# Two routed expert layers: all blocks of an expert in turn, odd 64 rows as half blocks, and jumps announced to TensorE's sequencer

## The chip, the cores and the metric

The kernel runs on one core of one Trainium2 chip. A core has five engines with an instruction queue each: TensorE (PE, matrix multiplications and transposes by matmul, with results in PSUM), VectorE (DVE), ScalarE (ACT), GpSimd (POOL) and SyncE (SP); sixteen DMA engines move data between HBM and the on-chip memory SBUF. Conditional code is executed by every engine for itself: each holds the condition in a register and jumps, or does not. The metric is the device time of one launch in microseconds (us); lower is better. About the trace: a float32 matmul is recorded as two passes.

## The reference

A stack of eight layers over 625 nodes with 512 features, four graph layers and four feed-forward layers alternating, each `x = x + layer(layernorm(x))`. Two feed-forward layers are routed: every node goes to its two best of eight experts. They are what the change rewrites:

```python
# L1: hidden 1024, bias and relu
topk_vals, topk_idx = jax.lax.top_k(x @ gate_w + gate_b, 2)
weights = sum over k of one_hot(topk_idx) * softmax(topk_vals)
out = sum over e of weights[:, e] * (relu(x @ w1[e] + b1[e]) @ w2[e] + b2[e])

# L3: hidden 1536, gated, no bias
probs = softmax(x @ router_w.T)
gates, idx = jax.lax.top_k(probs, 2); gates = gates / sum(gates)
out = sum over e of combine[:, e] * ((silu(x @ w1[e].T) * (x @ wgate[e].T)) @ w2[e].T)
```

The numbers of nodes per expert follow from the seeded inputs: L1 96, 346, 175, 23, 54, 50, 350, 156; L3 197, 240, 352, 99, 77, 43, 149, 93. The kernel does not know them when it is built.

Another layer the change touches is L1's graph layer, two rounds of graph attention. In it, VectorE also has time, and the degree normalisation of the adjacency matrix `aT` (needed in the graph layers of L2 and L3) can be placed anywhere between.

## The kernel before

Nodes are held as 5 tiles of 125. A routed layer has three parts.

**Routing.** `dispatch` (L514) turns the one-hot choices `o12` of the two best experts into slots. A triangular matmul gives each node its rank in its expert and `tot` the number of nodes. A slot is a place (0 to 127) in a block of 128 rows. Blocks 0 to 7 hold the first 128 rows of experts 0 to 7; rows beyond go to overflow blocks 8 to 16, filled in order of experts. One-hot matrices of place (`ohp`) and block (`ohb`) give by matmuls (`ps_id`) the table `node[place, block]` and, in three bf16 pieces, the weights `gate`. `whose` and `routing` say for each overflow block which expert it belongs to, and how many there are.

**Blocks.** `routed` (L619) works on a ring of 11 chunks of weights, 1 MB each, filled by SP (`refill`). Experts have 4 chunks in L1 (two for w1, two for w2) and 9 in L3 (three pairs for w1 and wgate, three for w2). For a block, POOL gathers its 128 rows from HBM (`fetch`, L667), PE transposes them (`enter`, L674), and for each part c of 512 hidden features `ahead` (L1170 in L1, L1335 in L3) multiplies with the upward weights into `ps_h`, `turn` (L688) transposes the hidden rows and `back` (L697) multiplies with the downward weights into `ps_y`. At its end DVE scales by the gate (L703) and POOL adds the rows to `sums` in HBM by an indirect DMA (L705). All code is emitted in one order per engine: `ahead` of unit n, `turn` of unit n-1, `back` of unit n-2, and the entry of the next block in between, over all first blocks without a gap.

Overflow blocks stand in conditionals nested in each other:

```python
with tc.If(n_over > i):
    run([(E + i, c) for c in range(nch)], i + 1 < NO)
    overflow(i + 1)
```

L1 uses 6 and L3 uses 5 of the 9 that the code holds. For an overflow block SP reads from a register which expert's weights to fetch and loads them once more (L654), by conditional DMAs.

A conditional that is not taken has code of its own: each engine waits until its earlier instructions are complete and then raises the semaphores that the skipped instructions would have raised.

**Beside them.** In L1's first units a list of other work (`fill`) is worked off, three items per unit: copies of `x` into `sums` (`keep`, L738), the experts' second bias for all nodes by five matmuls with the gate weights (`expert_bias`, L472), and the degree normalisation of `aT` for the graph layers of L2 and L3 (`normalise`, L1195).

Of the kernel before, what the change touches and what calls it, by code (L numbers as in the profile page):

```python
# [36 lines left out]
TMORE = 3  # L37
# [6 lines left out]
NB = 17  # L44
NO = NB - E
# [31 lines left out]
def _weights(i):  # L77
# [15 lines left out]
    for e in range(E):  # L93
        a, g = _chunks(i["L3_ffn_w1"][e].T), _chunks(i["L3_ffn_wgate"][e].T)
        for c in range(3):
            w += [a[c], g[c]]
        w += _chunks(i["L3_ffn_w2"][e].T)
# [55 lines left out]
def kernel(  # L153
# [51 lines left out]
    def load(w, src):  # L205
        nc.sync.dma_start(w.rearrange("p k m -> p (k m)"), src)
# [307 lines left out]
    def dispatch(layer, o12, weight, w0, per):  # L514


        with tc.tile_pool(name=f"{layer}d", bufs=1) as dp:
# [4 lines left out]
            rank, tot = ps[:T, 0, :NT * E], ps[:, 1, :E]  # L522
            nc.tensor.matmul(rank, tri, mask.rearrange("p t e -> p (t e)"), start=True, stop=False,
# [6 lines left out]
            for s in range(NT):  # L530
                nc.tensor.matmul(tot, ones16, mask[:, s, :], start=(s == 0), stop=(s == NT - 1))
            gt = dp.tile([P, E, 4], F32, tag="gt", name="gt")
            nc.vector.tensor_tensor(gt, tot[:, :, None].to_broadcast([P, E, 4]),
                                    thr[:, None, :].to_broadcast([P, E, 4]), op=OP.is_gt)
            nov = dp.tile([P, E], F32, tag="nov", name="nov")
            nc.vector.tensor_reduce(nov, gt, axis=AX.X, op=OP.add)
            pm = dp.tile([P, E, E], F32, tag="pm", name="pm")
            nc.vector.tensor_mul(pm, before, nov[:, None, :].to_broadcast([P, E, E]))
            ovb = dp.tile([P, E], F32, tag="ovb", name="ovb")
            nc.vector.tensor_reduce(ovb, pm, axis=AX.X, op=OP.add)  # L540
            delta = dp.tile([P, E], F32, tag="delta", name="delta")
            nc.vector.scalar_tensor_tensor(delta, ovb, float(B), dconst, op0=OP.mult, op1=OP.add)
            rk = rank.rearrange("p (t e) -> p t e", e=E)
            sl = dp.tile([T, NT, E], F32, tag="sl", name="sl")
            nc.vector.scalar_tensor_tensor(sl, rk, float(B),
                                           delta[:T, None, :].to_broadcast([T, NT, E]),
                                           op0=OP.is_ge, op1=OP.mult)
            nc.vector.tensor_add(sl, sl, rk)
            nc.vector.tensor_add(sl, sl, e128[:T, None, :].to_broadcast([T, NT, E]))
# [13 lines left out]
            ohp = dp.tile([T, 2 * NT, B], BF16, tag="ohp", name="ohp")  # L563
            ohb = dp.tile([T, 2 * NT, NB], F32, tag="ohb", name="ohb")
            nc.vector.tensor_tensor(ohb, blk[:T, None, :].to_broadcast([T, 2 * NT, NB]),
                                    bcast(at[:, 1, :], NB), op=OP.is_equal)
            nums = dp.tile([T, 2 * NT, NB, 2], BF16, tag="nums", name="nums")
            num = number.rearrange("p c t i -> p (c t) i")
            for i in range(2):
                nc.vector.tensor_mul(nums[:, :, :, i], ohb, bcast(num[:, :, i], NB))  # L570
            ps = pstile("ps_id")
            for n in range(2 * NT):
                nc.vector.tensor_scalar(ohp[:, n, :], place[:T, :], at[:, 0, n:n + 1], None,
                                        op0=OP.is_equal)
                nc.tensor.matmul(ps[:, 0, :2 * NB], ohp[:, n, :],
                                 nums[:, n].rearrange("p b i -> p (b i)"), start=(n == 0),
                                 stop=(n == 2 * NT - 1))
            one = dp.tile([P, NB], F32, tag="one", name="one")
            nc.vector.tensor_reduce(one, ps[:, 0, :2 * NB].rearrange("p (b i) -> p b i", i=2),
                                    axis=AX.X, op=OP.add)  # L580
            free = dp.tile([P, NB], F32, tag="free", name="free")
            nc.vector.tensor_scalar(free, one, 0.0, spare, op0=OP.is_equal, op1=OP.mult)
            node = small.tile([P, NB], I32, tag="node", name="node")
            nc.vector.scalar_tensor_tensor(node, one, -1.0, free, op0=OP.add, op1=OP.add)

            nc.vector.tensor_add(ovb, ovb, nov)
            le = dp.tile([P, NO, E], F32, tag="le", name="le")
            nc.vector.tensor_tensor(le, ovb[:, None, :].to_broadcast([P, NO, E]),
                                    blk[:, :NO, None].to_broadcast([P, NO, E]), op=OP.is_le)
            own = dp.tile([P, NO], F32, tag="own", name="own")  # L590
            nc.vector.tensor_reduce(own, le, axis=AX.X, op=OP.add)
            nc.vector.tensor_scalar(own, own, float(E - 1), None, op0=OP.min)
            whose = small.tile([P, NO, E], F32, tag="whose", name="whose")
            nc.vector.tensor_tensor(whose, own[:, :, None].to_broadcast([P, NO, E]),
                                    eio[:, None, :].to_broadcast([P, NO, E]), op=OP.is_equal)
            routing[layer] = small.tile([1, NO + 1], I32, tag="own_i", name="own_i")
            nc.vector.tensor_scalar(routing[layer][:, :NO], own[0:1, :], float(per), float(w0),
                                    op0=OP.mult, op1=OP.add)
            nc.vector.tensor_copy(routing[layer][:, NO:], ovb[0:1, E - 1:])

            rest = dp.tile([T, 2 * NT], F32, tag="rest", name="rest")
            nc.vector.tensor_copy(rest, weight)
# [14 lines left out]
        return node, gate, whose  # L617

    def routed(layer, node, gate, nch, nw, hidden, turned, first_fill=(), fill=()):  # L619
# [3 lines left out]
        w0, per = (W_L1, 4) if layer == "L1" else (W_L3, 9)  # L623
        assert state["taken"] == state["loaded"] == state["stop"]
        with tc.tile_pool(name=f"{layer}w", bufs=1) as more, \
# [9 lines left out]
            slots = kpool.tile([P, NT, D], F32, tag="K", name="slots")  # L635
            xgs = [slots[:, n, :] for n in range(3)]
            ys_out = [slots[:, n, :] for n in range(3, 5)]
            xgTs = [rpool.tile([P, KD, B], F32, name=f"xgT{n}") for n in range(2)]
            brought = {"n": 0}
            read = set()  # L640
            first = {}
            hs, hTs, ys = {}, {}, {}

            def bring(n):

                b, j = divmod(n, per)
                if b < E:
                    load(ring[n % RING], weights[w0 + n])
                    return
                if b not in first:  # L650
                    first[b] = nc.sync.value_load(routing[layer][0:1, b - E:b - E + 1],
                                                  min_val=w0, max_val=w0 + per * (E - 1))
                src = weights[bass.ds(first[b] + j, 1)].rearrange("a p m -> (a p) m")
                nc.sync.dma_start(ring[n % RING].rearrange("p k m -> p (k m)"), src,  # L654
                                  cond=n_over > b - E)

            def refill():

                while brought["n"] < NB * per:
                    n = brought["n"]  # L660
                    if n >= RING and n - RING not in read:
                        return
# [680 lines left out]
    def l3_turned(hT, pt, c, b, pool):  # L1343
        evac(hT, pt)
# [35 lines left out]
```

## Time and profile before

| What | Value |
|---|---|
| median of 3 runs (lowest to highest) | 1725.51 us (1724.1 to 1725.95) |
| the profiled execution | 1723.04 us |
| its span in the trace | 1721.1 us |
| granted clock of TensorE over the span | 0.936 of full speed |
| L1: `node` written, first `ps_h`, end of last `ps_y` | 786.2, 793.8, 1018.0 us |
| L3: `node` written, first `ps_h`, end of last `ps_y` | 1271.5, 1282.1, 1708.4 us |
| weights moved, L1 and L3 | 14 x 4 and 13 x 9 chunks of 1 MB |

The page of a profile gives the span, the busy time of each engine, the chain of work that ended last, followed back from the last instruction, and the costliest groups of instructions. A group's line reads: line of the kernel, engine, operation, output and input with their shapes, count, then busy time and mean duration of one in nanoseconds, then the idle time of the engine just before them and what ended it. A row of a table by window gives its bounds and length, each engine's busy time, the granted clock, the busy share of the DMA engines and the GB/s that they moved. A row for one line of the kernel gives shortest, median and longest duration in nanoseconds.

### The profile page before, as it was taken

To read this page: it belongs to the slowest core of one execution; us is meant where nothing else is said; L and a number is where in the kernel's file an instruction comes from. 1 tells how busy PE (TensorE), PEld (TensorE's weight loads), DVE (VectorE), ACT (ScalarE), POOL (GpSimd) and SP (SyncE) were. 2 spreads that over 40 slices of the span, in tenths; PEclk is the share of its full clock that TensorE was granted. 3 is DMA by queue.
4 is the path that set the end of the run, shared out by engine and by line. 5 is a ranking of instruction groups with operands and counts; after the bars stand their busy time and mean duration, and the time that the engine had idled before them with its cause. 6 is when DMAs were issued, how large, how long until landed. Compare 5 with 4: busy or idle time off the path is not lost.

```text
span 1721.1 us, 15559 instructions
## 1 busy us (share of the span) xinstructions
PE 1528.4 (89%) x5642; PEld 861.3 (50%) x5642; DVE 676.1 (39%) x1738; ACT 357.8 (21%) x680; POOL 235.5 (14%) x254
## 2 busy tenths in 40 slices
PE   7996999989897989846999969698759999999997
PEld 5774466555555656533444436354534444444443
DVE  9824562451974168466122225635331111111110
ACT  1102362011661046311111115301211000000100
POOL 2010042010540034101111112001000000000000
PEclk8998999999999989977999989799869999999998
DMA  3000200011001100136889731011258888869871
GB/s 135 16 28 25 73 1 25 31 68 53 22 1 49 49 26 1 40 112 234 302 270 342 256 87 73 25 49 49 102 217 299 301 309 304 307 244 359 311 265 50
DMA packets 40142, 237.12 MB, mean 138 GB/s; under 512 B 4779, under 2 KB 4907, under 8 KB 14299
## 3 DMA queue, kind: packets, MB, share of 16 engines
q1 hardware_dynamic: 30705, 214.80, 33.7%
q0 software_dynamic: 6608, 15.99, 4.1%
q10 hardware_dynamic: 2746, 5.25, 1.0%
q8 instruction: 48, 0.79, 0.2%
q14 instruction: 35, 0.29, 0.1%
HBM read 246.11 MB, written 14.26 MB: 151 GB/s over the span
## 4 chain that ended last, share of the span: by engine, by line
PE 70%; DVE 12%; issue 10%; DMA 4%; ACT 2%; POOL 1%; SPq 0%; POOLq 0%; ACTq 0%; DVEq 0%
PE ps_mf L359 17%; PE ps_y L697 9%; PE ps_h L1335 9%; PE ps_mn L367 7%; PE ps_h L1170 5%; PE ps_s L796 4%; PE ps_eo L496 4%; PE ps_o L860 3%; DMA sumsL<-slots,node 3%; PE ps_p L839 3%; PE ps_tr L328 2%; DVE ln_st L277 1%; DVE s L802 1%; PE ps_t L688 1%; DVE dst L913 1%
## 5 line engine op out<-in xcount | busy, mean ns | idle before, releaser
L1335 PE MATMUL ps_h<-ring,xgT 128*128 128x512 f32 x624 | 274.8, 595 | 0.8 <-DVE xgT L226 0.8
L697 PE MATMUL ps_y<-ring,hT 128*128 128x512 f32 x536 | 239.2, 593 | 0.9 <-issue 0.9
L1335 PEld LDWEIGHTS ps_h<-ring,xgT 128*128 128x128 f32 x624 | 118.7, 191 | 147.9 <-issue 145.3
L697 PEld LDWEIGHTS ps_y<-ring,hT 128*128 128x128 f32 x536 | 97.6, 190 | 103.9 <-issue 103.0
L825 POOL TENSOR_SCALAR s<-s,rs 125x625 f32<-125x625 f32 (+4 forms) x120 | 103.2, 875 | 294.0 <-DVE rs L822 269.9
L705 POOL DMA_INDIRECT sumsL<-slots,node x27 | 42.6, 1578 | 469.3 <-DVE slots L703 358.6
L1338 ACT ACTIVATE g<-ps_h 128x512 f32<-128x512 f32 x39 | 23.3, 597 | 395.6 <-PE ps_h L1335 364.5
L1170 PE MATMUL ps_h<-ring,xgT 128*128 128x512 f32 x224 | 103.2, 609 | 2.1 <-ACT xgT L234 1.3
L807 ACT ACTIVATE s<-s,mn 125x626 f32<-125x626 f32 (+4 forms) x120 | 87.2, 743 | 49.3 <-DVE mn L802 49.1
L802 DVE CUSTOM_DVE_ANT_0 s<-ps_s,mask 125x626 f32<-125x626 f32 (+4 forms) x120 | 82.6, 718 | 29.0 <-PE ps_s L796 27.8
L796 PE MATMUL ps_s<-kT,qT 64*125 64x313 f32 (+4 forms) x416 | 86.4, 466 | 2.8 <-DVE mn L802 2.8
L328 PE MATMUL ps_tr<-ident,xn 125*128 125x125 f32 x140 | 30.2, 398 | 62.6 <-DVE ln_nb L300 49.1
L226 DVE COPY hT<-ps_t 128x512 f32<-128x512 f32 x26 | 18.0, 692 | 171.5 <-PE ps_t L688 171.5
L1340 DVE TENSOR_TENSOR h<-ps_h,g 128x512 f32<-128x512 f32 x39 | 26.8, 686 | 147.9 <-ACT g L1338 147.9
L839 PE MATMUL ps_p<-ident,s 125*125 125x125 f32 x432 | 65.8, 293 | 14.0 <-POOL s L825 11.7
L359 PE MATMUL ps_mf<-xT,w 128*128 128x313 f32 x256 | 69.7, 434 | 6.6 <-ACT xT L402 6.6
L839 PEld LDWEIGHTS ps_p<-ident,s 125*125 125x125 f32 x432 | 53.9, 194 | 40.0 <-POOL s L825 28.6
L1170 PEld LDWEIGHTS ps_h<-ring,xgT 128*128 128x128 f32 x224 | 43.6, 196 | 57.5 <-issue 53.8
L817 DVE SCALAR_TENSOR_TENSOR s<-s,cnt 125x626 f32<-125x626 f32 x80 | 67.3, 863 | 9.9 <-ACT s L807 9.9
L496 PE MATMUL ps_eo<-w,h 128*125 128x512 f32 x160 | 70.6, 592 | 0.0
L860 PE MATMUL ps_o<-pT,v 125*64 125x375 f32 (+2 forms) x448 | 60.1, 413 | 9.0 <-DVE mn L802 4.2
L916 PE MATMUL ps_a<-dst,src 125*128 125x313 f16 x400 | 58.0, 309 | 6.9 <-DVE dst L913 5.3
(345 smaller groups left out, 1994.8 us busy)
## 6 DMA issues: line engine op xcount, KB each, us to landing
ring<-in_weights SPq DMA_DIRECT2D x195, 1024.0 KB
w<-in_weights SPq DMA_DIRECT2D x27, 1024.0 KB
rows_hbm<-xn ACTq DMA_DIRECT2D x2, 1120.0 KB
sumsL<-x ACTq DMA_DIRECT2D x2, 1120.0 KB
out<-sumsL SPq DMA_DIRECT2D x1, 1250.0 KB
x<-in_x SPq DMA_DIRECT2D x1, 1120.0 KB
x<-sumsL SPq DMA_DIRECT2D x5, 224.0 KB
rows<-in_rows SPq DMA_DIRECT2D x1, 1052.0 KB
```

The costliest lines, as they stand in the source:

```text
L359: nc.tensor.matmul(ps[:, half, :HC], w, r[:, half * HC:(half + 1) * HC], start=(n == 0), stop=(n == last))
L367: nc.tensor.matmul(ps[:T, 0, :width], src[:, k, t * T:(t + 1) * T], w[:, k, :width], start=(k == 0), stop=(k == KD - 1 and extra is None))
L496: nc.tensor.matmul(ps[:T, 0, :], h[:, t * T:(t + 1) * T], w, start=(f == 0), stop=(f == len(blocks) - 1))
L697: nc.tensor.matmul(ys[b][:, 0, :], hT[:, j, :], ring[n % RING][:, j, :], start=(c == 0 and j == 0), stop=(c == nch - 1 and j == 3))
L796: nc.tensor.matmul(ps[hh][:T, i, :w], qT[rr, b, t * T:(t + 1) * T], kT[rr, b, i * w:(i + 1) * w], start=True, stop=True)
L802: nc.vector.tensor_tensor_reduce(s[:, hh, :nb * w].rearrange("p (a c) -> p a c", a=nb), ps[hh][:T, :nb, :w], mask[:, t, :nb * w].rearrange ...
L807: nc.scalar.activation(s[:, hh, :nb * w], s[:, hh, :nb * w], AF.Exp, bias=mn[:, hh:hh + 1], scale=-1.0, accum_out=sm[:, hh:hh + 1] if caus ...
L825: nc.gpsimd.tensor_scalar(s[:, hh, :w], s[:, hh, :w], rs[:, hh:hh + 1], 1.0, op0=OP.mult, op1=OP.mult)
L839: nc.tensor.transpose(pp[:T, hh, j * T:(j + 1) * T], s[:, hh, j * T:(j + 1) * T], ident[:T, :T])
L860: nc.tensor.matmul(po[rr, 0, o:n * T], v[:, j, h * DH:(h + 1) * DH], pT[:, hh, j, o:n * T], start=(j == 0), stop=(j == nk - 1))
L1170: nc.tensor.matmul(ps[:, 0, :], xgT[:, k, :], w1[:, k, :], start=(k == 0), stop=(k == KD - 1))
L1335: nc.tensor.matmul(ps[:, i, :], xgT[:, k, :], w[i][:, k, :], start=(k == 0), stop=(k == KD - 1))
```

## The change

Both routed layers are rewritten, with one code for both.

- Experts come in straight line, each with all its blocks while its weights are in the ring. Weights are loaded once: 32 MB instead of 56 in L1, 72 instead of 117 in L3. The loads into chunks that a block has read are conditional: they run in the expert's last block alone. The ring has 12 chunks, and in L3 the order of the nine chunks is another.
- An expert has 48 / 8 = 6 block columns. If the number of its half blocks of 64 rows is odd, the first 64 rows are a half block (`l = 0`); all others are full blocks, `l = 1` and, nested, `l = 2` to `5`. In a half block the hidden features (and the output's) are split in two: two matmuls with stationary tiles of 64 columns and 256 moving columns each, on PSUM partitions 0 to 63 and 64 to 127. Its result goes by half rows (`by_half`) to `sums`.
- For each expert, `enter(e + 1)` transposes the next expert's first rows (128 and 64 of them) before this expert's blocks, and then gathers those of the expert after that. Rows of further blocks are gathered one block ahead, and transposed at the start of their block.
- In each block's code `hint` marks, on TensorE alone, that the jump over the blocks behind it is likely taken. The jumps over a half block and over block 1 have no such mark of their own.
- Counts and oddness of all experts, 16 numbers, are read into registers of all engines at the start of the layer.
- `dispatch`: no overflow table; numbers of nodes in one fp16 matmul instead of two bf16 parts; 48 columns instead of 17; the first gathers are issued as soon as `node` is written. In L3 the softmax over eight is gone: the weights come from the difference of the two best logits, as in L1. L1's second bias is now computed here, with copies on ACT (`added`), and added to `x` at its end.
- The degree normalisation is emitted in the projections of the second round of L1's graph layer, two steps per evacuation.

Taken blocks for these counts: in L1 9 full and 5 half, in L3 11 full and 2 half.

The diff at its core:

```diff
-TMORE = 3
+TMORE = 4
...
-NB = 17
-NO = NB - E
+NL = 6
+NB = E * NL
+BH = B // 2
...
-        for c in range(3):
-            w += [a[c], g[c]]
-        w += _chunks(i["L3_ffn_w2"][e].T)
+        d = _chunks(i["L3_ffn_w2"][e].T)
+        w += [a[0], g[0], a[1], g[1], d[0], a[2], g[2], d[1], d[2]]
...
+    def load(w, src, cond=None):
+        nc.sync.dma_start(w.rearrange("p k m -> p (k m)"), src, cond=cond)
...
+            ci = dp.tile([P, E], I32, tag="ci", name="ci")
+            nc.vector.tensor_scalar(ci, tot, 1.0, float(BH - 1), op0=OP.max, op1=OP.add)
+            odd = dp.tile([P, E], I32, tag="odd", name="odd")
+            nc.vector.tensor_scalar(odd, ci, BH, None, op0=OP.bitwise_and)
...
+            xg(node)
+            routing[layer] = number_of.rearrange("p a e -> p (a e)")
+            nc.vector.tensor_copy(number_of[:, 0, :], tot[0:1, :])
+            nc.vector.tensor_copy(number_of[:, 1, :], odd[0:1, :])
...
+            def fetch(e, node):
+                if e < E:
+                    gather(xg_block, node, e, 1)
+                    gather(xg_half, node, e, 0)
+
+            refill()
+            node, gate, node2, gate2 = dispatch(layer, lg, lambda node: fetch(0, node), bias)
+            _, numbers = nc.values_load_multi_w_load_instructions(routing[layer], min_val=0,
+                                                                  max_val=N)
+            counts, odd = numbers[:E], numbers[E:]
...
+            def enter(e):
+                if e < E:
+                    turned(xg_block, xbT[e % 2])
+                    turned(xg_half, xhT[e % 2])
+                    fetch(e + 1, node)
...
+                    n = 1 if l else 2
+                    self.parts = [(slice(g * B // n, (g + 1) * B // n),
+                                   slice(g * 512 // n, (g + 1) * 512 // n)) for g in range(n)]
+                    self.width = 512 // n
...
+                    self.cond = counts[e] < B * l + BH + 1 if l < NL - 1 else None
...
+                def ahead(self, c):
+                    ps, n = pstile("ps_h"), self.width
+                    for i, w in enumerate(up[c]):
+                        w = chunk_of(self.e, w)
+                        for k in range(KD):
+                            for rr, cc in self.parts:
+                                nc.tensor.matmul(ps[rr, i, :n], self.xT[:, k, :], w[:, k, cc],
+                                                 start=(k == 0), stop=(k == KD - 1))
...
+                def run(self):
+                    read.clear()
+                    read.update(before[0])
+                    brought["n"] = before[1]
+                    for n in range(nch + 2):
+                        if n < nch:
+                            self.ahead(n)
+                        if 1 <= n <= nch:
+                            self.turn(n - 1)
+                        if n >= 2:
+                            self.back(n - 2)
+
+            def hint(e, l):
+                if l < NL:
+                    tc.mark_branch_hint_location(f"{layer}e{e}b{l}", "LikelyTaken",
+                                                 engines=[mybir.EngineType.PE])
+
+            def more(e, l):
+                if l < NL:
+                    with tc.If(counts[e] > B * l - BH, label=f"{layer}e{e}b{l}"):
+                        hint(e, l + 1)
+                        turned(xg_more, xbT[e % 2])
+                        if l + 1 < NL:
+                            gather(xg_more, node, e, l + 1)
+                        Block(e, l).run()
+                        more(e, l + 1)
+
             enter(0)
-            run([(b, c) for b in range(E) for c in range(nch)], True)
-            assert not fill
-            overflow(0)
+            for e in range(E):
+                before = set(read), brought["n"]
+                enter(e + 1)
+                with tc.If(odd[e] > 0):
+                    hint(e, 2)
+                    Block(e, 0).run()
+                with tc.If(counts[e] > BH):
+                    hint(e, 2)
+                    gather(xg_more, node, e, 2)
+                    Block(e, 1).run()
+                more(e, 2)
...
+    routed("L1", lg, ((0,), (1,)), (2, 3), vec("L1_ffn_b1"), b2s[:E, 1, :])
...
+    lg = node_logits(xnT, vec("L3_ffn_router_w"), None, "lg")
+    routed("L3", lg, ((0, 1), (2, 3), (5, 6)), (4, 7, 8))
```

## The prediction

> **What bounds the kernel now.** I read the page first: span, busy time, and the chain that ended last.
>
> ```profile
> span 1721.1 us, 15559 instructions
> PE 1528.4 (89%) x5642; PEld 861.3 (50%) x5642; DVE 676.1 (39%) x1738; ACT 357.8 (21%) x680; POOL 235.5 (14%) x254
> PE 70%; DVE 12%; issue 10%; DMA 4%; ACT 2%; POOL 1%; SPq 0%; POOLq 0%; ACTq 0%; DVEq 0%
> ring<-in_weights SPq DMA_DIRECT2D x195, 1024.0 KB
> ```
>
> TensorE leads. The two routed stages, which the change rewrites, are then cut out by time (columns: window, length, busy time of PE, its loads, DVE, ACT and POOL, granted clock, DMA share, GB/s): L1 is the first three rows, L3 the last three.
>
> ```profile
> 764.00:794.00 30.00, 11.39 (x76) 8.28 (x77) 19.51 (x96) 7.77 (x12) 4.37 (x7) 0.61 0.33 112
> 794.00:915.00 121.00, 119.01 (x340) 56.77 (x341) 34.96 (x73) 17.23 (x42) 15.55 (x13) 0.97 0.87 301
> 915.00:1018.00 103.00, 102.05 (x292) 48.61 (x290) 23.83 (x69) 14.26 (x36) 17.06 (x13) 1.00 0.64 222
> 1245.00:1282.00 37.00, 14.31 (x75) 8.99 (x75) 18.12 (x93) 6.86 (x11) 3.32 (x4) 0.55 0.52 187
> 1282.00:1515.00 233.00, 232.85 (x623) 109.02 (x624) 28.18 (x43) 20.70 (x36) 16.03 (x13) 0.99 0.85 300
> 1515.00:1711.00 196.00, 193.42 (x523) 90.31 (x521) 24.75 (x36) 16.53 (x29) 16.00 (x12) 1.00 0.71 256
> ```
>
> Inside the expert stretches PE is busy 98 to 100% at nearly full clock: DMA, though 64 to 87% busy, isn't the limit, so fewer weight bytes save nothing by themselves. Ahead of each stretch lies a routing stretch at 0.55 to 0.61 clock, in which DVE leads. Next, groups by shape, and the jumps of the conditional blocks:
>
> ```profile
> L1335 PE MATMUL ps_h<-ring,xgT 128*128 128x512 f32 x624 | 274.8, 595 | 0.8 <-DVE xgT L226 0.8
> L697 PE MATMUL ps_y<-ring,hT 128*128 128x512 f32 x536 | 239.2, 593 | 0.9 <-issue 0.9
> L1170 PE MATMUL ps_h<-ring,xgT 128*128 128x512 f32 x224 | 103.2, 609 | 2.1 <-ACT xgT L234 1.3
> L860 PE MATMUL ps_o<-pT,v 125*64 125x250 f32 x240 | 28.7, 379 | 7.0 <-DVE mn L802 4.2 <-ACT pT L841 1.7 <-DVE pT L226 1.1
> L730 PEldq COMPARE_BRANCH  x15: 65/65/3839, 920.3 to 1708.6; - x15
> L730 POOLq INC_SWDGE_SEM  x2: 858/1120/1383, 1019.5 to 1709.7; - x2
> ```
>
> An fp32 matmul is two records, 0.429 us apart at full clock: 0.857 us per 512 columns; a 128x128 transpose takes 0.107. From the first ps_h to the last ps_y, L1's 14 blocks take 224.2 us (793.8 to 1018.0), L3's 13 take 426.3 (1282.1 to 1708.4). From one block's first ps_h to the next's, overflow blocks take 15.4 and 32.66 us; less four entry transposes (0.43) that is 14.97 and 32.2.
>
> [...]the ps_o matmuls of attention (L860) are such pairs on partitions 0 to 63 and 64 to 127; both start within 0.01 us and the next pair 0.21 us later, as long as one 250-column pass; the change of mode shows as about 0.05 us. [...]of 15 branches 13 fall through in 0.065 us, L1's exit over 271 instructions takes 0.352, L3's over 722 takes 3.839. [...]L1's first eight ps_h records took 5.33 us where later ones took 3.43.
>
> **The change, part by part**, for the counts that the seeded inputs give: L1 96, 346, 175, 23, 54, 50, 350, 156; L3 197, 240, 352, 99, 77, 43, 149, 93.
>
> *Fewer rows.* L1's 14 full blocks become 9 full and 5 half; L3's 13 become 11 and 2. A half block's 16 (L1) or 36 (L3) pairs cost 2 x 0.214 us each: 6.9 or 15.4; with transposes (0.4 or 0.6) and about 1.0 of evacuations that nothing covers, as a block no longer overlaps its neighbour, 8.3 and 17.1. So L1: 9 x 14.97 + 5 x 8.3 = 176.2; L3: 11 x 32.2 + 2 x 17.1 = 388.4.
>
> *Entries.* enter(e+1) for the six experts from e2 on: 8 transposes with 128 and 64 rows, 0.64 us: 3.9 per stage. The blocks of `more` (4 in each stage) transpose their rows with no other PE work beside: four transposes 0.43, copy 0.69 (L226), semaphores: 1.7 each, 6.8 per stage.
>
> *Blocks not taken.* The old kernel leaves an If twice; the new one leaves 14 times in L1 and 15 in L3. At L1's exit PE's sequencer branched at 1012.3, but its semaphore event waited until PE's own matmuls were through (1018.08), and it went on at 1018.41. I charge 1.15 us (0.85 dead plus waits refilling the pipe) for the first false block of a run and 0.85 to 0.9 for the others: 7 x 1.15 + 2 x 0.9 + 3 x 0.85 = 12.4 in L1, 7 x 1.15 + 5 x 0.9 + 0.85 = 13.4 in L3 (the false blocks behind the last expert are in both kernels). Bounds: 0.4 to 1.8 each, so 10 to 50 for all.
>
> *The announced jumps* (L1 376 to 385, L3 742 to 756 instructions): once announced, 0.35 as at L1's exit. Even unannounced most lie under the 6 us of queued matmuls that hid L3's 3.8; worth 0 to 10. *The unannounced ones*: a skipped half block is 141 to 148 instructions in L1 and 309 to 319 in L3. The latter happens at six experts (e0, e1, e2, e3, e4, e7) with only entry transposes queued ahead. [...]0 to 3.5 each, 0 to 21; I take 4, since the shorter jump of 271 cost 0.35.
>
> *POOL.* Two gathers per expert, one more in each full block, fewer scatters; on a false block POOL waits for its scatter to land (6.6 us median) and for the increment (0.86 to 1.38). Behind a full block that is covered by 15 us or more. Behind L1's half-only e3, e4, e5 (about 11 us each) landing, increment, two gathers and their landing (7.0 median) come to 17: three stalls of up to 6. I take 8 for L1 (0 to 18), 1 for L3. PE cools in these: 2 per stage. SP, in a false block, waits for its loads to land; only later loads are queued behind it, and at least three chunks are in the ring by then, 5 us of a half block's or 10 of a full block's use against 3.0 to 3.4 us per load: nothing, or about 3 per stage where that cover is gone.
>
> Sums: L1 176.2 + 3.9 + 6.8 + 12.4 + 8 + 2 = 209.3 against 224.2: -14.9. L3 388.4 + 3.9 + 6.8 + 13.4 + 4 + 1 + 2 = 419.5 against 426.3: -6.8.
>
> *The start of each stage.* enter(1) stands ahead of expert 0's blocks, and the gathers of expert 1 wait for expert 0's transposes to free the buffer. Before, L1 goes node 786.2, first landing 791.8, first ps_h 793.8. After: node about 786.7, two gathers down by 794.3, transposes, then two more gathers down by 802, ps_h at 803.5: +9.7. In L3 the first gather took 7.7 us beside ring loads that are now issued earlier, and the softmax is gone: +5 (4 to 9). Reading 16 counts (one value 0.26 to 0.54 us now) hides under the first gather on every engine; uncovered at most 4.
>
> *Elsewhere.* The degree normalisation (21 DVE and ACT steps) moves from L1's first units to the L1-gnn projections of its second layer, under PE work; 0 to +3, I take +1. The bias matmuls move into routing, where PE idles. The ring's 12th chunk and the new order of L3's chunks change what DMA holds in reserve, not a wait: DMA must bring 32 MB instead of 56, and 72 instead of 117. Removed DVE routing steps are in the node times above.
>
> Total: -14.9 - 6.8 + 9.7 + 5 + 1 = -6.0. From the profiled execution (1723.04, span 1721.1 and 1.9 around it) that gives 1717.0; that execution lies 2.5 below the median, and put on the median 1725.5 it is 1719.5. I forecast 1719.
>
> **Rivals.** *Overheads hide* (0.27): false blocks cost 0.5[...]. Minus 13 on drains, 8 + 1 + 4 on stalls, gives 1693 to 1705, say 1698. For it: PE's sequencer ran 6 us ahead. Against: both observed exits drained.
>
> *Skipped half blocks miss* (0.16, slower): [...]21 instead of 4, and L1's three (e0, e1, e6) half that, +5: 1741. It decides from two misses on: beyond the 4 charged, 6 us eat the gain. For it: 722 instructions missed[...]. Against: 271 did not.
>
> *Gathers become the path* (0.15, slower): each false block holds POOL for its scatter at every L1 expert, not three, and PE waits 5 us at six of eight and cools: +24, 1743. Against: the full block's cover.
>
> *The announcement does nothing* (0.04): 1719 to 1729, as worked out.
>
> **How the numbers follow.** The sum stands at 0.38, with its own range of 1708 to 1731. About 0.2% (3.5 us) is what a measurement of this kernel can tell from no change. Of the main case 0.25 lies under 1722, 0.09 within, 0.04 above; the hiding rival is all faster, the misses and the gathers nearly all slower, the last mostly within. Faster 0.53, same 0.12, slower 0.35. Cases of both signs hold most of the chance; 1690 to 1750 leaves 2 in 10 out.
>
> **What would show it.** First ps_h 15 to 20 us after node in L1 and L3, with two rounds of gathers between (right) or 7 to 10 (wrong). Half blocks 8 and 17 us with paired starts 0.21 us apart. PE's branches: announced ones at most 0.4, the odd ones of L3 0.1 to 0.4 (right) or near 3.8 (the miss). PE idle before transposes ended by gathers: 8 us in L1, or over 25. Weight loads 104 with 1 MB landing, DMA share below 0.6. It would be wrong if PE's idle per expert is far from 3 us, or if a chunk of weights is late.

## The result and the profile after

The changed kernel takes 1796.5 us (median of 4 runs, 1790.7 to 1798.5) against 1725.1: the ratio is 1.041, 95% interval 1.038 to 1.043. The forecast was 1719, in a range of 1690 to 1750: 77 us off, and on the other side of the kernel before.

The page of the changed kernel, at its head, its instruction fetches, its costliest group, and the weight loads:

```profile
span 1796.8 us, 17242 instructions
PE 1515.9 (84%) x5966; PEld 865.3 (48%) x5966; DVE 670.8 (37%) x1697; ACT 382.1 (21%) x709; POOL 255.7 (14%) x275
...
q8 instruction: 80, 1.31, 0.3%
...
L761 PE MATMUL ps_h<-ring,xbT 128*128 128x512 f32 x672 | 315.3, 627 | 63.1 <-SPq L854 41.3
...
ring<-in_weights SPq DMA_DIRECT2D x158, 1024.0 KB
```

PE was busy for 12.5 us less than before, in a span 75.7 us longer. The idle time ahead of one group, the upward matmuls, is 63.1 us, and what ended most of it is SyncE's queue at L854, the `If` of the half block. The packets on q8, one of the two queues that the page marks "instruction", rose from 48 to 80. (Of the 158 issues of weight loads, 54 took about 0.08 us where the others took 0.33: they are conditional loads that did not run. 104 ran, as forecast.)

By stage, from the records of the two traces, in us (`node` is taken at the start of the instruction that writes it; the three stretches marked * were forecast at +1 together):

| Stretch | before | after | difference | predicted |
|---|---|---|---|---|
| start to L1's logits transposed (`ps_lt`) | 775.2 | 779.9 | +4.7 | * |
| L1: logits to `node` | 10.8 | 11.4 | +0.6 | +0.5 |
| L1: `node` to first `ps_h` | 7.8 | 18.8 | +11.0 | +9.2 |
| L1: first `ps_h` to last `ps_y` | 224.2 | 225.5 | +1.3 | -14.9 |
| to L3's logits | 241.5 | 240.1 | -1.4 | * |
| L3: logits to first `ps_h` | 22.6 | 27.8 | +5.2 | +5 |
| L3: first `ps_h` to last `ps_y` | 426.3 | 479.9 | +53.6 | -6.8 |
| to the end | 12.7 | 13.4 | +0.7 | * |

So the two starts were forecast nearly right, and the expert stretches were wrong by 16 and 60 us. The windows of these two stretches, first before, then after (columns as in the prediction):

```profile
793.80:1018.00 224.20, 221.26 (x631) 105.59 (x631) 58.99 (x141) 31.48 (x78) 32.81 (x26) 0.99 0.77 265
1282.10:1708.40 426.30, 426.25 (x1144) 199.33 (x1144) 52.08 (x77) 37.23 (x65) 30.42 (x24) 1.00 0.79 282
```

```profile
810.10:1035.60 225.50, 195.03 (x764) 98.27 (x764) 39.28 (x91) 27.62 (x78) 39.68 (x36) 0.94 0.43 133
1303.50:1783.40 479.90, 417.10 (x1288) 197.00 (x1288) 51.22 (x81) 61.44 (x85) 38.44 (x32) 0.93 0.42 148
```

The rows saved are there: PE's busy time falls by 26 us in L1 and 9 in L3, although the granted clock is 0.93 to 0.94 there and was 0.99 to 1.00. Idle time took their place: 63 us of L3's stretch, 30 of L1's. That is 7.9 us per expert in L3, where the prediction named "far from 3 us" as a sign of being wrong. What ended it in L3 is told by TensorE's waits from 1300 to 1790 us (who waits, for whom; sum, times, longest; a q behind an engine's name is its instruction queue, where jumps and semaphores are worked off):

```profile
PE ps_h L761 <- SPq L854: 37.6, 4, 9.8
PE ps_h L761 <- PEq L854: 10.9, 2, 6.1
PE ps_h L761 <- SPq L842: 6.7, 2, 3.8
PE ps_x L718 <- DVEq L842: 5.5, 5, 1.1
```

L842 is the `If` of the nested blocks (`more`), L854 that of the half block. Ahead of experts 1, 2, 3 and 4, whose half block is skipped, PE stands still for 9.8, 9.3, 9.5 and 9.1 us. One of these pauses, ahead of expert 1, in the timeline:

```profile
1373.71 0.33 SPq L206 DMA_DIRECT2D ring<-in_weights  x1
...
1374.78 1.02 PE L718 MATMUL ps_x<-ident,rows_g 128*128 128x128 f32 x8 [1.10 <-DVEq L842]
...
1385.57 2.04 PE L761 MATMUL ps_h<-ring,xbT 128*128 128x512 f32 x2 [9.77 <-SPq L854]
```

The last weight load of expert 0 is issued at 1373.7, when its last chunk has been read. In the DMA view of 1373 to 1386 us, slices of 0.325 us, the engines carry about 400 GB/s and more up to 1379 us and less than 100 from 1384.4 on (rows are gathered and added in it too):

```profile
GB/s 454 403 429 429 429 454 429 479 403 429 429 454 429 403 403 403 378 429 227 353 359 410 271 365 277 227 227 315 353 391 410 265 214 126 164 63 76 25 0 0
```

SyncE's own waits in the same stretch:

```profile
SPq L842 <- SPq L842: 10.2, 5, 4.3
```

Its records fit: in the nested block not taken its semaphore events come at 1375.2, 1377.7, 1380.3 and 1384.5 us, 2.5 to 4.3 us apart, then those of the half block not taken until 1385.5, and PE starts at 1385.6. Each of the four comes within 0.03 us of the end of a landing (1375.16, 1377.65, 1380.24 and 1384.50). So SyncE, skipping a block, waits here until the loads it has issued have landed, and PE's next expert waits for SyncE.

A second wait lies under the first. TensorE's jumps at these places (COMPARE_BRANCH is the instruction that jumps or falls through; rows of L3, from 1285 to 1790 us; shortest, median and longest in ns):

```profile
L842 PEldq COMPARE_BRANCH  x15: 69/351/2166, 1333.0 to 1777.6; - x15
L854 PEldq COMPARE_BRANCH  x10: 75/4219/6570, 1297.9 to 1744.7; - x10
L857 PEldq COMPARE_BRANCH  x15: 82/186/237, 1303.1 to 1777.3; - x15
```

Of the announced jumps taken (L842), seven of eight take 0.35 to 0.37, and the one behind expert 5's half block 2.2. Those over a half block, six of the ten at L854, take 4.9, 5.9, 6.6, 6.2, 6.0 and 3.5 us; within each of the six one packet of 16 KB starts on q8 (that the jump waits for it is not shown). In the timeline above TensorE's jump ran from 1375.1 to 1381.0, still inside SyncE's wait.

### The profile page after: what moved, and what is told of

The parts are those of the page before. It is cut to its first block, busy times and chain, and to the rows that moved or that the text cites. A ratio compares the mean times of both kernels' runs of the same rounds, so it can differ in the third digit from the quotient of the medians.

```text
span 1796.8 us, 17242 instructions
## 1 busy us (share of the span) xinstructions
PE 1515.9 (84%) x5966; PEld 865.3 (48%) x5966; DVE 670.8 (37%) x1697; ACT 382.1 (21%) x709; POOL 255.7 (14%) x275
## 5 line engine op out<-in xcount | busy, mean ns | idle before, releaser
L761 PE MATMUL ps_h<-ring,xbT 128*128 128x512 f32 x672 | 315.3, 627 | 63.1 <-SPq L854 41.3
L761 PEld LDWEIGHTS ps_h<-ring,xbT 128*128 128x128 f32 x672 | 132.9, 202 | 226.1 <-issue 215.0
L804 PE MATMUL ps_y<-ring,hT 128*128 128x512 f32 (+1 forms) x664 | 209.8, 511 | 0.0
L804 PEld LDWEIGHTS ps_y<-ring,hT 128*128 128x128 f32 (+1 forms) x664 | 92.7, 169 | 92.2 <-issue 83.4
L733 POOL DMA_INDIRECT sumsL<-rows_g,node x27 | 43.1, 1598 | 577.3 <-DVEq L842 297.3
L769 DVE TENSOR_TENSOR h<-ps_h,g 128x512 f32<-128x512 f32 (+1 forms) x39 | 25.2, 647 | 253.6 <-ACT g L768 253.6
L953 PE MATMUL ps_p<-ident,s 125*125 125x125 f32 x432 | 67.2, 298 | 13.0 <-POOL s L939 10.2
L694 POOL DMA_INDIRECT rows_g<-rows_hbm,node x52 | 50.1, 964 | 149.3 <-DVE gates L628 73.1
L732 DVE TENSOR_SCALAR rows_g<-ps_y,gate 128x512 f32<-128x512 f32 (+1 forms) x27 | 18.4, 682 | 137.0 <-PE ps_y L804 137.0
L359 PEld LDWEIGHTS ps_mf<-xT,w 128*128 128x128 f32 x256 | 50.7, 199 | 27.5 <-ACT xT L402 7.1
L910 PEld LDWEIGHTS ps_s<-kT,qT 64*125 64x125 f32 x416 | 45.6, 191 | 30.1 <-DVE mn L916 9.5
```

Of the source, the lines that this page charges most:

```text
L359: nc.tensor.matmul(ps[:, half, :HC], w, r[:, half * HC:(half + 1) * HC], start=(n == 0), stop=(n == last))
L761: nc.tensor.matmul(ps[rr, i, :n], self.xT[:, k, :], w[:, k, cc], start=(k == 0), stop=(k == KD - 1))
L804: nc.tensor.matmul(self.y[ro, 0, :n], hT[:, j, rr], w[:, g * nj + j, co], start=(c == 0 and g == 0 and j == 0), stop=(c == nch - 1 and g = ...
L910: nc.tensor.matmul(ps[hh][:T, i, :w], qT[rr, b, t * T:(t + 1) * T], kT[rr, b, i * w:(i + 1) * w], start=True, stop=True)
L953: nc.tensor.transpose(pp[:T, hh, j * T:(j + 1) * T], s[:, hh, j * T:(j + 1) * T], ident[:T, :T])
```

## The experiments

All times are medians of four or more runs; the kernel before was at 1724 to 1726 beside each. "Pauses" are the idle times of PE ahead of the first `ps_h` of experts 1, 2, 3, 4 and 7 in L3.

**e1: no loads in the blocks.** In `done`, `refill(self.cond)` is taken out, in both layers.

> The changed kernel without any weight load inside the blocks: the first 12 chunks stay in the ring and serve every expert (so the values are those of other weights; the work of every other engine is the same). Theory A: in L3 the pause ahead of each expert with a skipped half block (9.1 to 9.8 us in the changed kernel) is set by SyncE, which in the block not taken waits until its weight loads have landed, and whose raise the first ps_h waits for. Then the pauses fall to what TensorE's own jump costs, about 6.3 us, the pauses of 3.8, 1.3, 2.9 and 2.8 us around experts 5 and 6 mostly go, and the time is 22 to 35 us below the changed kernel: 1762 to 1775. Theory B: TensorE's jump over the skipped half block (4.9 to 6.6 us) alone sets them. Then at most 8 us are gained: 1788 or more.

Measured: 1693.4, ratio 0.982 (0.980 to 0.983). Far more than either theory, but only in part for their reason: with L1's values changed, L3's routing changed, and the experts took other paths (396.7 us). L1 is comparable, and fell from 225.5 to 210.0 (in other traces with the changed kernel's code up to there, e2, e3, e7, e12 and e14, it took 226.6 to 230.0); the prediction's sum was 209.3. The run that settles L3 is e7.

**e2: no half block's code where it is skipped.**

```diff
+                if not (layer == "L3" and e in (0, 1, 2, 3, 4, 7)):
                     with tc.If(odd[e] > 0):
```

> The code of the half block is left out in L3 for the six experts whose half block is skipped anyway (0, 1, 2, 3, 4, 7); what is computed stays the same. This takes away TensorE's jump of 309 to 319 instructions and SyncE's raises for that block's loads together. Theories A and B both expect the six pauses (6.1, 9.8, 9.3, 9.5, 9.1, 4.7 us) to fall to 1.5 to 2 us and the colder clock after them to go (about 2 us each): 40 to 50 us less, 1747 to 1757. If neither is right, and the pause is an expert change as such, the time stays above 1785.

Measured: 1743.2 (ratio 1.010, 1.008 to 1.013), 53 us less than the changed kernel and a little more than expected. The pauses at the skipped half blocks are gone; L3's stretch takes 428.5 us.

**e3: the half block keeps only its loads** for the same experts: in place of `Block(e, 0).run()`, `done(i)` is called for each chunk.

> For the same six experts of L3 the half block's code keeps its weight loads and loses everything else, so TensorE jumps over a handful of instructions and SyncE's part stays as it was; what is computed stays the same, as these blocks are skipped. Theory A (SyncE's raise sets the pause): the five pauses stay at 8.5 to 9.8 us, the first one (6.1 us at expert 0) goes, as SyncE was long through there: 5 to 12 us less, 1785 to 1792. Theory B (TensorE's jump): all six fall to 1.5 to 2 us, 1747 to 1757.

Measured: 1789.5, 7 us less; the intervals of the two ratios (1.035 to 1.038 here) just touch. The jumps and waits of L3:

```profile
L854 PEldq COMPARE_BRANCH  x9: 75/221/236, 1367.4 to 1741.1; - x9
PE ps_h L761 <- SPq L854: 28.2, 3, 10.2
PE ps_h L761 <- SPq L842: 15.0, 4, 9.5
```

TensorE's jumps are 0.22 to 0.24 us, and the pauses ahead of experts 1 to 4 are still 9.2, 8.9, 9.5 and 10.2, all ended by SyncE. Theory A: SyncE sets them, the jump lies underneath.

**e4: no announcements.** `hint` does nothing.

> The changed kernel without the announcements to TensorE's sequencer. If they work as the shorter jumps suggest (0.2 to 0.4 us where 4 to 6 are paid unannounced), the jumps over the nested blocks rise to 4 to 6 us; behind full blocks these lie under about 6 us of matmuls still queued, so the loss is small there, and about 2 us more at each of the four half-only experts: 0 to +15 us, 1796 to 1811. If on the contrary [...]the jumps over the half blocks get cheaper without it, and the time falls by up to 15.

Measured: 1799.6 against 1796.5, ratios to the kernel before 1.044 (1.042 to 1.045) and 1.041 (1.038 to 1.043). The intervals overlap, so a gain of the announcement is not shown in the time. In the trace the announced jumps are shorter:

```profile
L842 PEldq COMPARE_BRANCH  x15: 65/442/7478, 1326.9 to 1774.4; - x15
```

Six of these jumps take 6.4 to 7.5 us without it in L3; with it five of the same took 0.35 to 0.37 and one 2.2. But behind a full block PE still has about 6 us of matmuls queued (in the changed kernel the jump at 1367.6 starts 6.1 us before the semaphore event that waits for them, at 1373.7), and most of the 6.4 lay under those. Behind expert 5's half block there is no such queue, and PE waited 8.1 us instead of 2.8. The second part of the expectation, jumps over half blocks getting cheaper, holds clearly for one of six (0.35 at expert 3).

**e5: the next expert's rows are transposed at its own start** (`enter(e)` for `enter(e + 1)`, no `enter(0)` ahead).

> An expert's first rows are transposed at its own start, not at that of the expert before, so the first block waits for one round of gathers and not for two. What is computed stays the same. By the prediction's step on the start of a stage the first ps_h comes 6 to 7 us earlier after node in L1 and 3 to 5 in L3 (there the jump of 4.9 us took over from the gathers); each later expert pays the copy of its rows after the transposes, about 1 us, where no wait of 9 us covers it: L1 +4 to +8, L3 0 to +4. Together 5 us less to 3 us more: 1791 to 1800. If the second round of gathers had been hidden, 6 to 12 us more.

Measured: 1794.6, within the noise of 1796.5. The first `ps_h` comes 14.3 instead of 18.8 us after `node` in L1 and 12.6 instead of 17.3 in L3; L1's stretch grew by 2.3 and L3's by 7.6. So taking the second round of gathers away brought 4.5 us in L1, less than the 6 to 7 expected, as a wait of 3.5 for TensorE's jump took part of its place; and the other order gives it back, with more loss in L3 than the 0 to 4 expected.

**e6: without the degree normalisation** (`normalise()` is not called).

> The changed kernel without the 25 steps of the degree normalisation (left out, so the graph layers of L2 and L3 work on plain counts, and L3's routing may differ; the part up to L1's last ps_y is that of the changed kernel). If these steps, in the projections of L1's graph layer, delay the evacuations, the end of L1's logits comes 4 to 6 us earlier (in the changed kernel it came 4 us later than before the change). If the delay has another source, less than 1 us.

Measured: 1797.9. L1's logits come at 777.2 us instead of 779.9, but in kernels with the same code up to there they came anywhere from 775.3 (e3, e7) to 779.9. Inconclusive; nor can the 4.7 us by which they came later than in the kernel before be put down to the change's code.

**e7: no loads in L3's blocks**, L1 as it was.

> As the run without reloads, but in L3 alone, so that L1's output and L3's routing stay those of the changed kernel (L3's values are those of the first 12 chunks). In the run without reloads TensorE's jumps over skipped half blocks had become 0.35 to 0.45 us instead of 4.9 to 6.6; if it is the weight traffic that makes the instruction fetch slow, that holds here too: L3 from first ps_h to last ps_y takes 420 to 428 us instead of 479.9, and the time is about 1796 - 56 = 1740 (1735 to 1745). If the short jumps there came from the other path through the experts, jumps stay at 5 to 6 us once SyncE's wait is gone: L3 at about 450 us, time about 1765.

Measured: 1754.0 (ratio 1.018, 1.015 to 1.021), L3 at 435.0, between the two cases expected. The pauses are 3.4, 1.7, 1.7, 1.7 and 4.7. Jumps were short (0.34 to 0.47) at experts 2, 3 and 4 and long (3.6, 3.9) at 1 and 7, without any weight loads in the blocks, so this traffic alone is not what decides. This opened the question of the instructions' places.

**e8: the loads moved out of the half block**, into straight line behind the expert's blocks:

```diff
                     read.add(self.e * per + i)
-                    refill(self.cond)
+                    if self.l:
+                        refill(self.cond)
...
                 more(e, 2)
+                read.clear()
+                read.update(before[0])
+                brought["n"] = before[1]
+                read.update(range(e * per, (e + 1) * per))
+                refill(counts[e] < BH + 1)
```

> A half block loads no weights any more; those that follow a half-only expert are issued, conditionally, in straight line behind the expert's blocks. What is computed stays the same. The first ps_h of an expert then depends on SyncE's work of two experts ago. Theory A (two waits lay over each other, SyncE's of 9 to 10 us and the jump's of 5 to 6.6): the pauses at L3's five skipped half blocks fall to the jump, 5.5 to 6.5 us, the pauses inside the half blocks of experts 5 and 6 change little: 12 to 25 us less, 1772 to 1785. Theory C (any raise of SyncE's is late, wherever its loads stand): pauses stay at 9 us, less than 8 us gained.

Measured: 1753.8 (1.016, 1.014 to 1.018), 43 us less; L3 442.7. Pauses 6.2, 1.7, 1.7, 1.7, 1.5: SyncE's wait has gone from them, and at experts 2 to 4 the jump is short too, though nothing was done to it. More than theory A expected. Ahead of expert 1 the jump itself took 0.44 us, and the view of waits names a weight load (`DMA ring<-in_weights`, 6.2); but TensorE's queue stood still from 1371.9 to 1377.6 us ahead of a branch that waits for no semaphore, so that the stall there looks like that of a jump, one instruction later. L1's stretch is 221.7.

**e9: as e8, and the next half block's jump announced as well**, in each block.

> The run before, and each block also announces the jump over the next expert's half block. If TensorE's sequencer keeps two announced targets, L3's six jumps of 309 to 319 instructions fall from 5 to 6.6 us to 0.4, and the pauses with them to about 1.5: 25 to 35 us less than the run before, about 1750. If it keeps one target[...], no gain, or the nested jumps rise to 4 to 6 us again (mostly under queued matmuls): within 8 us of the run before.

Measured: 1775.1 (1.027, 1.023 to 1.030), 21 us more than e8. The jumps at experts 1 to 4 take 6.2 to 6.6 us, the nested ones still about 0.35. So the second announcement brought nothing where it was needed. In the trace the two announcements of a block follow each other within 0.1 us. Why the second brought nothing is not shown: the added instructions also shift TensorE's later ones, which matters by itself (e14).

**e10 and e13: as e8, shifted.** 53 (e10) or 55 (e13) matmuls of one column, unused, ahead of L3's first transposes, move TensorE's later instructions by 212 or 220. The question is whether the length of a jump hangs on its place in the program.

> The run with the loads moved out, and 53 tiny matmuls (one column each, unused) ahead of L3's first transposes, where TensorE waits for gathers: they only shift its later instructions by 212. [...]experts 0 and 1, the two that still stalled (5.9 and 6.2 us), fall to about 1 and 1.7, with the colder clock behind them: 8 to 13 us less, 1741 to 1746. If the short jumps came from the moved loads, no change: 1750 to 1757.

Measured: 1751.5 (1.015, 1.013 to 1.017), not distinguishable from e8. The jumps of experts 0 to 4 are 0.36 to 0.46 us and the pauses ahead of experts 0 and 1 fell from 5.9 and 6.2 to 1.8 and 1.7; but ahead of expert 7 a nested jump took 6.4 and the half block's 2.9, and L3's stretch took 444.3 us against 442.7. Experts 0 and 1 came out about as expected, expert 7 stayed long. Two more shifts were chosen, 220 (e13) and 168 (e14). "The rule" that they go by is an estimate of the author's from positions counted in the program; no trace shows it:

> The shifted run with the loads moved out, shifted by 8 instructions more (55 tiny matmuls). [...]all six at 0.3 to 0.5 us, the pause ahead of expert 7 falls from 4.6 to 1.5 or 3, and the time by 1 to 4 us: 1747 to 1751. If the rule is wrong, one or more of the first five stalls again, 4 to 6 us each, or expert 7's stays at 2.9.

> The changed kernel, its loads where they were, with 42 tiny matmuls ahead of L3's first transposes, which shift TensorE's later instructions by 168. By the rule all six jumps over skipped half blocks fall from 3.5 to 6.6 us to 0.3 to 0.5. SyncE's wait stays, so the four pauses ahead of experts 1 to 4 stay at 9 to 10 us (theory A); only expert 0's 6.1 and expert 7's 4.7 shrink, by 4 and 3: 5 to 9 us less than the changed kernel, 1788 to 1792. If the jumps had set the pauses after all, 1760.

**e14** is the changed kernel itself with 42 such matmuls, its loads where they were. Measured: e13 1746.5 (1.013, 1.011 to 1.015), e14 1790.5 (1.038, 1.036 to 1.040). The branch rows of L3, first of e13 (L859 is the half block's `If` there), then of e14 (L858):

```profile
L859 PEldq COMPARE_BRANCH  x10: 75/395/627, 1292.2 to 1698.2; - x10
```

```profile
L858 PEldq COMPARE_BRANCH  x10: 75/338/904, 1300.3 to 1746.0; - x10
```

No half block's jump is above 0.91 us in either; that of expert 7 is the longest in both (0.63 and 0.90), the others take 0.33 to 0.47. In time, e13 is not clear of e10's noise. And e14's waits in L3 show SyncE's part left alone:

```profile
PE ps_h L761 <- SPq L858: 38.0, 4, 10.0
PE ps_h L761 <- SPq L842: 6.9, 3, 3.3
```

With e9 this makes a square: time, and in brackets L3's stretch, in us, with the windows of e13 and e14 below:

| | SyncE's wait in | SyncE's wait out |
|---|---|---|
| half block's jumps long | 1796.5 [479.9] (the change) | 1775.1 [460.6] (e9, four of six long) |
| half block's jumps short | 1790.5 [478.8] (e14) | 1746.5 [438.7] (e13) |

```profile
1293.30:1732.00 438.70, 411.49 (x1288) 193.97 (x1288) 51.21 (x81) 61.50 (x85) 39.51 (x34) 0.97 0.46 163
1301.50:1780.30 478.80, 417.85 (x1288) 197.01 (x1288) 51.20 (x81) 61.48 (x85) 39.47 (x34) 0.93 0.43 150
```

In L3's stretch either wait taken away alone gives 1 or 19 us, both together 41: they overlap. The times say the same less cleanly: e9 and e13 have their loads moved in L1 too (its stretch is 225.1 and 220.5), and e14's runs (1787.4 to 1795.5) are not clear of the change's (1790.7 to 1798.5). In e14 a nested jump behind expert 5's half block took 4.9 us instead of 2.2, which gave part of the gain back.

**e11: the attempt at a better kernel.** As e10, with two sets of row buffers, so that experts 0 and 1 are gathered together, a ring of 11 chunks, and one normalisation step per evacuation in both rounds of L1's graph layer.

> The run before (shifted, loads moved out) with two sets of row buffers, so that the gathers of experts 0 and 1 are issued together (the ring is back at 11 chunks for the space), and the normalisation's steps spread over both rounds of L1's graph layer, one per evacuation. The first ps_h comes 5 to 7 us earlier after node in each routed layer, and L1's logits 1 to 4 us earlier: 12 to 18 us less than the run before, 1725 to 1732, which is the kernel before the change, not better. If the ring of 11 is too short, 3 to 6 us of that are lost in L3's last experts.

Measured: 1747.0 (1.013, 1.011 to 1.015), about 4 us less than e10, not 12 to 18. The first `ps_h` comes 14.3 us after `node` in L1 (18.8 in e10) and 11.3 in L3 (14.5 in e10), 4.5 and 3.2 earlier where 5 to 7 were expected; L3's stretch grew by 3 us and L1's logits came at 782.1. The 4 us are not clear of noise. No run with the change's results beats the kernel before (e1 is faster, but computes something else). What e13 still loses, by its trace, lies in L3's stretch (12.4 us more than before) and in L1's start from the logits to the first `ps_h` (11.6 more).

**e12: the floor.** L3 with neither the skipped half blocks' code nor loads in its blocks.

> L3 with neither of the two causes: no weight loads in its blocks (its values are those of the first 12 chunks), and no code for the half blocks that are skipped (in the changed kernel and here, six of eight). It shows what L3's new order costs by itself. Without the skipped halves alone, L3 took 428.5 us, of which 9 were pauses for chunks in experts 5 and 6; so 417 to 422 here, which is 4 to 9 us below the kernel before (426.3) and near the prediction's sum (419.5); the whole about 1728 to 1738, as L1 and the later start stay. If L3 stays at 426 or more, the prediction's prices for an expert change were too low by themselves.

Measured: 1732.8 (1.005, 1.003 to 1.006). The window of L3's stretch:

```profile
1295.30:1715.20 419.90, 404.92 (x1288) 194.06 (x1288) 50.07 (x79) 59.65 (x85) 40.31 (x34) 0.99 0.10 20
```

PE is busy for 404.9 of 419.9 us at 0.99 of its clock: without the two causes the new order is 6.4 us faster than before in L3. That this is near the prediction's 419.5 is partly luck: that sum also holds 4 us for jumps and about 5 for the six skipped half blocks, which e12 does not have, so what e12 does run took about 10 us more than it was charged.

## Why the prediction was wrong, step by step

*SyncE.* This is the step that failed. The prediction said that SP, in a false block, waits for its loads to land, and that "only later loads are queued behind it", to be covered by the chunks in the ring: nothing, or about 3 us per stage. The first half is right. The second overlooks who waits for SP: in the code a full block of an expert reads the ring after the half block's loads into it, so its first matmul waits for those loads' semaphores even where they were skipped, and SP raises these only after its landing wait. The price was 9 to 10 us at each of four experts. With the jumps short, moving the loads out of the half blocks was worth 40 us of L3's stretch (e14 to e13).

*The unannounced jumps.* Charged 4 us, bounds 0 to 21. They took 33 us in all (six of 3.5 to 6.6), more than the one long jump of the kernel before (3.8) had suggested as a ceiling. In the changed kernel they were worth 1 us of L3's stretch (e14) and 3 of its start (24.4 instead of 27.8), as most lay under SyncE's wait; without that wait four of them were worth 22 of the stretch (e9 less e13). The rival "skipped half blocks miss" named a real stall at the right place and the wrong cause of the time.

*L3's sum.* 419.5 was forecast, 479.9 measured. From the trace: pauses at five skipped half blocks 42.4 (9.8 + 9.3 + 9.5 + 9.1 + 4.7); waits inside experts 5 and 6, and at the change between these experts, 10.8: 3.8 and 2.9 ended by SyncE, which was waiting for landings in blocks not taken there too, 2.8 by a nested jump, and 1.3 by nothing that the trace names. The six full blocks behind the pauses lasted 34.1 to 35.3 us from first `ps_h` to last `ps_y` instead of 32.5, with the clock at 0.5 for 3 to 14 us around each pause: 13.3 together. That is 66.5 where the sum had 7 (4 for jumps, 1 for POOL, 2 for the clock), 60 too little. The other terms were off by less and nearly cancel: a full block took 32.5 where 32.2 was charged, the two half blocks 38.6 without their waits where 34.2, and what else lies between blocks 17 where 24.1 was charged for entries and blocks not taken. The clock's mean over the stretch is 0.93 where it was 1.00 before.

*L1's sum.* 209.3 forecast, 225.5 measured, and 210.0 in e1: row prices, drains and stalls were right in sum (a full block took 15.4 us where 14.97 was charged, and the stalls for gathers were smaller, see below), and the 15.5 us hang on the weight loads: one pause of 3.7 that SyncE ended, a lower clock (0.94 on average, 0.99 before), and jumps behind the half-only experts 3, 4 and 5 (4.3, 2.6 and 1.8 us with loads, 1.4, 0.3 and 1.8 without), though announced 9 to 14 us ahead.

*The starts* were right within 2 us, L3's in part by luck: it holds a jump of 4.9 us that was charged elsewhere, and where that jump took 0.33 (e14) the start was 24.4 us, under the 27.6 forecast. *The announcement* was right behind L3's full blocks (0.35 to 0.37) and worth little under queued matmuls; at other places "at most 0.4" was wrong: 2.2 behind L3's half block at expert 5, and 1.8 to 4.3 at five of L1's eight. *Paired half blocks* were right: in e12 expert 5's half block runs without a pause for 17.3 us, where 17.1 was forecast. *Gathers as the path* did not come about: after the first block PE's waits for gathered rows come to 2.5 us in L1 (8 were charged) and to none in L3. With the loads moved one such wait of 6.1 (e8) or 4.6 (e13) shows in L1.

*The lengths of jumps.* The same jumps over half blocks of L3 took 3.5 to 6.6 us in the change and 0.33 to 0.90 in e14, where TensorE's instructions lie 168 further on. The shifts of e13 and e14 go by the author's estimate, and their twelve jumps (0.33 to 0.90) came out nearly as forecast (0.3 to 0.5); what makes one place short and another long is not shown. Why announced jumps took 6.4 us in e10, 4.9 in e14 and 2 to 4 elsewhere, and what made L1's logits vary by 4 us, stays open.

## What to carry to other kernels

When code is made conditional, price the block not taken on every engine, the DMA-issuing one first: here skipping meant waiting for what it had in flight, and an asynchronous prefetch became a barrier for anyone who waited for a semaphore raised behind it (9 to 10 us at each of four experts). Keep prefetches out of conditional blocks that are often skipped, or see that nothing read next waits behind them. Where two waits overlap, take each away alone and both together before pricing them.

## What was not expected of the hardware

- A jump over about 310 instructions on TensorE took 0.33 to 0.47 us at most places in some runs and 3.5 to 6.6 at the same places in others, depending on where it lay: shifting the program by 168 instructions, with work that nothing uses, turned six long jumps into short ones (e14).
- A long jump cost up to 6.6 us beside weight loads at 400 GB/s, and 3.6 to 3.9 at the two long ones where there were none (e7).
- Each pause of about 9 us was followed by a block 1.6 to 2.8 us longer than one in a steady stretch.
